# A fused stage whose instruction order comes from a table of places in a turn, one for every occurrence of a step

## The chip, the cores and the metric

The kernel runs on one core of a Trainium2 chip. The metric is device time in microseconds (us) of one execution. Before the change the median of three runs is 1330.56 us (1325.54 to 1330.76).

Five engines take part, each with its own queue of instructions that it works off strictly in the order in which the program lists them: PE (matrix products, with PEld for its weight loads), DVE (vector), ACT (activation), POOL (GpSimd) and SP, which here only issues DMAs. An instruction that waits for another engine holds up all that stands behind it in its own queue. So the order of each queue, which is what this change sets, is part of the program and not of its computation.

## The reference, cut to what matters

The input `x` is 128 sequences of 64 tokens of 256 features. Two layers follow, each with a residual.

```python
h  = scan(gated recurrence over 64 steps of x)              # layer 0, first part
x  = x + ffn_int8(h)                                        # gate, up, silu, int8 fake quant, down
# layer 1, per token row of 256, hyperbolic geometry
xn = layer_norm(logmap0(x)); xm = expmap0(xn * (1 + sc) + sh)
q, k, v = plin(xm, w_q), plin(xm, w_k), plin(xm, w_v)       # 16 heads of 16, 64 x 64 scores
y  = mobius_add(x, expmap0(g * logmap0(attention(q, k, v))))
z  = mobius_add(y, expmap0(g2 * logmap0(plin(plin(modulated layer_norm(y), w_f1), w_f2))))
x  = x + fp6_quant(z) @ fp6_quant(weight).T + bias
```

Norms, `tanh` and `artanh` of a row are one number per row, so a large share of the instructions are chains of tiny ones on tiles of 128 x 8.

## The kernel before, in words

The 8192 tokens are 64 tiles of 128 rows. The program has three stages. The recurrence and the weight preparation come first, then the first part of the int8 feed-forward, which writes its product `h` to DRAM, and then the **fused stage**, the function `fused`, which does all the rest. The change touches the fused stage alone.

There the tiles go in 16 groups of 4 (`GT`, `NGR`). For every group five pieces of work are done: `front` (dequantise `h`, down projection, residual: the steps `load.h`, `front.q8`, `front.cast`, `front.mm`, `front.x1`, `front.add`, `stats1`), `norms` (`ln_coeffs`, `modulate`, the scale `chain.su` and `clip_ball`), `attention` (steps `a.*`), `mlp` (steps `m.*`) and `fp6` (steps `f.*`). `tail` closes the attention of one group and the mlp of another one in one set of tiny instructions (`tail_coeffs`, step `chain.tail`), since both have the same form, and `norms` likewise serves an attention group and an mlp group at once.

The loop at the end of `fused` runs turns k = -5 to 18. In turn k it traces `tail(k)`, `norms(k)`, `fp6(k - 3)`, `mlp(k)`, `attention(k + 5)` and `front(k + 6)`. So the loop is software pipelined: turns -5 to -1 fill the pipe, and turns 11 to 18 empty it. Many of the tiles between the pieces have one or two buffers. In PSUM the banks `dn`, `ao`, `ml` and `fp` are single, and `qk` and `sc` are double.

The order of the queues is not the order of the trace. A list scheduler of the language takes, in a simulated time line, among the instructions whose inputs are ready the one with the lowest priority number. `step(name)` sets this number for what is traced next: `base + (turn + 5) * 1800 + RANK[name]`. `RANK` has one number for each of some 80 step names, so all occurrences of a step in a turn (the eight `a.e`, the four `m.mm`) and all their instructions share one number. The scheduler remains free to deviate from it whenever it believes that an instruction isn't ready, and it does so differently in each turn.

Lines that the prediction speaks of: L774 (`q`, the first instruction of `tail_coeffs`), L651 (a power of -0.5 on POOL, `rsqrt`, used by `chain.tail`, `ln_coeffs`, `chain.su`, `chain.cf` and `chain.full`), L779 to L814 (the rest of `tail_coeffs`), L679 to L710 (`ln_coeffs`), L739 and L740 (`modulate` on DVE), L638 (`clip_ball` on DVE), L756 (the gate product on POOL), L764 (the row products `xdot`), L977 and L982 (`a.qk`, `a.va` on POOL), L940 (`a.lo` on DVE), L1064 (`a.proj`), L1163 (`f.add`).

Of the kernel before, what the change touches and what calls it, by code (L numbers as in the profile page):

```python
# [46 lines left out]
GT = 4  # L47
NGR = NTILE // GT

TURN = 1800  # L50
RANK = {"front.q8": 910, "front.cast": 539, "front.mm": -718, "front.x1": -1305, "front.add": 174, "store.x1": 0, "a.turn": -1220, "a.hi": -1577, "a.lo": 495, "a.qkv": 46, "a.qkvcopy": -917, "a.sq": 2253, "a.nh": -44, "chain.h": -8170, "a.qk": -90, "a.va": -90, "a.turnq": -90, "a.qm": -1178, "a.kt": -1474, "a.sc": -90, "a.e": -877, "a.av": -90, "a.raw": -1338, "a.o": 3284, "a.turno": 1011, "a.ot": -3468, "a.wo": 975, "a.proj": -2819, "m.turn": 987, "m.hi": -123, "m.lo": -2161, "m.mm": 1726, "m.dot": -468, "m.copy": 301, "m.a": -355, "f.max": -10889, "f.q": 4682, "f.rnd": -1889, "f.deq": 4033, "f.turn": 167, "f.yt": 4664, "f.mm": 507, "load.ot": 10015, "f.add": -588, "store.out": -58, "x2n": 2724, "own": 641, "load.xt": -636, "chain.su": 4117, "chain.full": -5861, "chain.cf": -1389, "chain.ln": -2069, "chain.tail": -2513, "stats1": 1067, "stats2": 339, "load.mod0": -1252, "load.mod1": -208, "mod0.0": -3294, "mod0.1": -93, "mod0.2": 398, "mod0.3": -712, "mod1.0": 1137, "mod1.1": 2275, "mod1.2": -5509, "mod1.3": 1054, "sqm0": 2326, "sqm1": -1277, "clip0": -1974, "clip1": -1974, "sqt0": 462, "sqt1": -162, "gate0": -1900, "gate1": 755, "sqg0": -808, "sqg1": 4262, "xdot.a": -1630, "xdot.m": 1293, "load.h": -5461, "load.x": 0, "a.sqo": 76, "load.gate0": 3865, "load.gate1": 3539, "comb.a": 708, "comb.m": -2849}

LA, LM = CFG["LA"], CFG["LM"]

# [510 lines left out]
def fused(ctx, tc, a, out_tok, x_tok, L):  # L565
    nc = tc.nc
    V, S, G_, PE = nc.vector, nc.scalar, nc.gpsimd, nc.tensor
# [21 lines left out]
        Q[CFG["q_" + key]].dma_start(out=out, in_=in_)  # L589

    at = [0]
    turn_ = [-LA]
    base = tc.cur_priority + 4000

    def step(name):

        tc.cur_priority = base + (turn_[0] + LA) * TURN + RANK[name]

    def mk(name, n=2 * GT, bufs=CFG["mk"]):

# [11 lines left out]
    def pick(key, g):  # L612

        es = CFG[key]
        if at[0] < CFG["ef"]:
            es = CFG["fill"].get(key, es)
        return es[g % len(es)]
# [51 lines left out]
    def ln_coeffs(mv, xs=None):  # L669


        step("chain.ln")
        k = lambda name, bufs=1: mk(f"{name}ln", bufs=bufs)
        m, v = mv[:, :, 0], mv[:, :, 1]
        x2s, aa = k("x2s", CFG["xs"]), k("lna", CFG["la"])
        t, rn, n_, l1, l2, z, p, far, near, l1q = (
            k(i) for i in ("t", "rn", "n", "l1", "l2", "z", "p", "far", "near", "l1q"))
        S.activation(t, m, AF.Square)
        V.tensor_tensor(t, t, v, ALU.add)  # L679
        if xs is not None:  # L680
            xx, vx = k("xx"), k("vx")
            S.activation(xx, xs, AF.Square)
            V.tensor_tensor(vx, v, xx, ALU.mult)
            V.tensor_tensor(t, t, xx, ALU.mult)
            v = vx
        V.tensor_scalar(x2s, t, float(D), EPS2, ALU.mult, ALU.max)


        V.tensor_scalar(z, x2s, 1.0 / 32.0, None, ALU.min)
        V.tensor_scalar(far, x2s, 1.0 / 32.0, 0.5, ALU.is_ge, ALU.mult)  # L690
        series(p, z, ARTANH)
        rsqrt(rn, x2s, "n")
        V.tensor_tensor(n_, x2s, rn, ALU.mult)
        V.tensor_scalar(n_, n_, MAX_T, None, ALU.min)
        S.activation(l1, n_, AF.Ln, bias=one, scale=1.0)
        S.activation(l2, n_, AF.Ln, bias=one, scale=-1.0)

        V.tensor_tensor(rn, rn, far, ALU.mult)
        S.activation(near, far, AF.Copy, scale=-2.0 * ARTANH[0], bias=ARTANH[0])
        V.scalar_tensor_tensor(p, p, 1.0 / ARTANH[0], near, ALU.add, ALU.mult)  # L700
        V.tensor_tensor(l1, l1, l2, ALU.subtract)
        V.tensor_tensor(l1, l1, rn, ALU.mult)
        V.tensor_tensor(l1, l1, p, ALU.add)

        S.activation(l1q, l1, AF.Square)
        V.reciprocal(t, l1q)
        V.scalar_tensor_tensor(t, t, 1e-6, v, ALU.mult, ALU.add)
        rsqrt(aa, t, "v")
        if xs is not None:
            V.tensor_tensor(aa, aa, xs, ALU.mult)  # L710
        return x2s, aa

# [14 lines left out]
    def modulate(src, nm, aa, which, i0, u, un):  # L727

        for g in range(GT):
            step(f"load.mod{which}")  # L730
            ss = load_ada(which, 0, 2, i0 + g)
            step(f"mod{which}.{g}")
            ug = u[g]
            if pick(f"mod{which}", g) == "G":
                G_.tensor_scalar(ug, src[g], nm[:, g : g + 1], aa[:, g : g + 1], ALU.add, ALU.mult)
                G_.tensor_tensor(ug, ug, ss[:, 1, :], ALU.mult)
                G_.tensor_tensor(ug, ug, ss[:, 0, :], ALU.add)
            else:
                V.scalar_tensor_tensor(ug, src[g], nm[:, g : g + 1], ss[:, 1, :], ALU.add, ALU.mult)  # L739
                V.scalar_tensor_tensor(ug, ug, aa[:, g : g + 1], ss[:, 0, :], ALU.mult, ALU.add)  # L740
            step(f"sqm{which}")
            square_sum(pick(f"sqm{which}", g), f"u{which}", ug, un[:, g : g + 1])

    def clip_ball(u, su, which):

        for g in range(GT):
            step(f"clip{which}")
            scale(pick(f"su{which}", g), u[g], u[g], su[:, g : g + 1])
# [18 lines left out]
    def tail_coeffs(ag2, xg, x2s, xs, own, src, cols):  # L767
# [3 lines left out]
        k = lambda name: mk(f"{name}tc")  # L771
# [22 lines left out]
        V.tensor_tensor(yc, e, r2[:, gt:], ALU.mult)  # L794
        S.activation(y2, e, AF.Square)
        if xs is not None:
            V.tensor_tensor(xg, xg, xs, ALU.mult)
        V.scalar_tensor_tensor(t1, xg, 2.0, yc, ALU.mult, ALU.mult)
        V.tensor_tensor(xy, x2s, y2, ALU.mult)
        V.scalar_tensor_tensor(den, t1, 1.0, xy, ALU.add, ALU.add)  # L800
# [3 lines left out]

        S.activation(t1s, t1, AF.Copy, bias=TINY)
        if xs is not None:
            V.tensor_tensor(t1s, t1s, xs, ALU.mult)
        V.tensor_tensor(s_, t1s, den, ALU.mult)
        if own is not None:
            S.copy(own[:, cols], s_[:, src])  # L810
        V.reciprocal(t1, t1s)
        S.activation(r, x2s, AF.Copy, scale=-1.0, bias=1.0)
        V.tensor_tensor(yc, yc, t1, ALU.mult)
# [39 lines left out]
    def get_mv(k):  # L853

        if k not in mvs:
            step("own")
            mvs[k] = mk("mv", 4 * GT, CFG["mv"]).rearrange("p (g k) -> p g k", k=2)
            if k < 0 or k + LA >= NGR:
                G_.memset(mvs[k], 1.0)
        return mvs[k]  # L860

    def get_tail(k):

        if k not in tails:
            step("own")
            t = tails[k] = mk("ag2", 4 * GT, CFG["tl"]), mk("xg", bufs=CFG["tl"]), mk("x2n", bufs=CFG["tl"])
            if not LM <= k < NGR:
                for v in t:
                    G_.memset(v, 1.0)
        return tails[k]  # L870
# [296 lines left out]
    def norms(k, xs):  # L1167

        on_a, on_m = k + LA < NGR, k >= 0
        mv = mvs.pop(k)  # L1170
        step("chain.ln")
        un, nm = mk("un"), mk("nm")
        if not (on_a and on_m):
            G_.memset(un, 1.0)
        x2n, la = ln_coeffs(mv, xs)
        S.activation(nm, mv[:, :, 0], AF.Copy, scale=-1.0)
        todo = []
        if on_m:
            um = ums[k] = Pairs("u2")
            todo.append((1, k, us[k], um, HM))  # L1180
        if on_a:
            ua = uas[k + LA] = Pairs("u1")
            todo.append((0, k + LA, x1s[k + LA], ua, HA))
        for which, i, x, u, h in todo:
            at[0] = i * GT
            modulate(x, nm[:, h], la[:, h], which, i * GT, u, un[:, h])
            if not CFG["jsu"]:
                clip_ball(u, radial(un[:, h], f"su{which}"), which)
        if CFG["jsu"]:
            su = radial(un, "su")  # L1190
            for which, i, x, u, h in todo:
                clip_ball(u, su[:, h], which)
        step("x2n")
        if on_a:
            G_.tensor_copy(get_tail(k + LA)[2][:, HA], x2n[:, HA])
        if on_m:
            G_.tensor_copy(get_tail(k + LM)[2][:, HM], x2n[:, HM])

    def tail(k):

# [29 lines left out]
            return u, s_[:, HM]  # L1230

    xss = {}
    for pr in range(CFG["hl"]):
        load_h(pr)
    for i in range(CFG["fl"]):
        front(i)
    for k in range(-LA, NGR + LM):
# [13 lines left out]
            fp6(k - LM, *done)  # L1251
        if k + LA + CFG["fl"] < NGR:
            front(k + LA + CFG["fl"])


# [46 lines left out]
```

## Time and profile before

| what | us |
| --- | --- |
| median of three runs | 1330.56 |
| the profiled execution's own time | 1332.73 |
| its span, first to last instruction | 1331.0 |
| DVE busy in the span | 1128.2 |
| PE busy | 1075.1 |
| ACT busy | 847.8 |
| POOL busy | 840.2 |

The profile is of one execution. The fused stage's engine work begins at about 302 us, where the first instructions of `front` start (the first loads of `h` are issued earlier). The turns can be told by L774, which occurs once in each of the turns 0 to 18. It starts at 461.9 us in turn 0 and at 1294.2 us in turn 18. The time axis of the views is microseconds from the span's start, and an engine's idle time before an instruction is put down to the instruction that ended its wait.

### The profile page before, as it was taken

Reading aid. Unit: us, or ns where it says so; the run is one execution under the profiler, and the core shown is the slowest. Engines: PE = TensorE matmul, PEld = TensorE weight load, DVE = VectorE, ACT = ScalarE, POOL = GpSimd, SP = SyncE. Lnnn points to the kernel's source line nnn. Section 1 sums busy time; section 2 is a strip of 40 time slices with the busy share of each in tenths; the row PEclk is TensorE's granted clock in tenths of the full one; section 3 lists DMA queues with packets and bytes.
Section 4 is the critical chain, followed back from the end, with each engine's and each line's share of the span. In section 5 each row is a group of like instructions: output and inputs, shape, how many; then the busy total and the mean of one; then the engine's idle time right before and its main releaser. Section 6 shows DMA issues by size and latency. Waiting matters only on the chain. (4 is left out here: it accounts for less than half of the span.)

```text
span 1331.0 us, 23828 instructions
## 1 busy us (share of the span) xinstructions
PE 1075.1 (81%) x7382; PEld 742.9 (56%) x7404; DVE 1128.2 (85%) x3337; ACT 847.8 (64%) x2607; POOL 840.2 (63%) x1024
## 2 busy tenths in 40 slices
PE   6999977984479798988889788897888988874756
PEld 5766642332356565655666566675666756653534
DVE  5766769995787779899999999999989999799674
ACT  2455547981467677678667776776778867764331
POOL 3110118864787858878968778776686776764541
PEclk9999979995699899899899899998999869986765
DMA  7721105678843314334335245323432223323211
GB/s 240 294 70 59 54 1 201 262 276 255 259 130 106 126 33 143 113 103 146 113 124 155 89 127 159 96 69 120 135 105 80 65 72 96 96 84 91 80 43 52
DMA packets 119304, 163.64 MB, mean 123 GB/s; under 512 B 10885, under 2 KB 72074, under 8 KB 119178
## 3 DMA queue, kind: packets, MB, share of 16 engines
q1 hardware_dynamic: 119178, 162.13, 38.5%
q8 instruction: 58, 0.95, 0.3%
q14 instruction: 68, 0.56, 0.1%
HBM read 115.94 MB, written 46.14 MB: 122 GB/s over the span
## 5 line engine op out<-in xcount | busy, mean ns | idle before, releaser
L629 ACT ACTIVATE junk<-u 128x256 bf16<-128x256 f32 x432 | 182.2, 425 | 102.8 <-POOL u L756 31.4
L950 PE MATMUL qk<-wqkv,uT 128*128 128x512 f32 (+1 forms) x768 | 180.2, 374 | 10.7 <-ACT uT L938 10.5
L756 POOL TENSOR_TENSOR u<-u,ada 128x256 f32<-128x256 f32 x128 | 100.0, 785 | 86.4 <-ACT junk L629 76.3
L950 PEld LDWEIGHTS qk<-wqkv,uT 128*128 128x128 f32 x768 | 126.1, 202 | 46.5 <-issue 17.6
L1007 PE MATMUL sc<-qM,kT 64*64 64x256 f32 x1024 | 126.7, 412 | 10.9 <-ACT kT L996 9.4
L1095 PE MATMUL ml<-wm,uT 128*128 128x512 f32 (+1 forms) x384 | 122.5, 458 | 0.0
L1095 PEld LDWEIGHTS ml<-wm,uT 128*128 128x128 f32 x384 | 84.7, 223 | 51.0 <-issue 14.7
L1026 PE MATMUL ao<-va,e 128*64 128x34 f32 x2048 | 89.5, 240 | 22.0 <-DVE u L1064 13.1
L1026 PEld LDWEIGHTS ao<-va,e 128*64 128x64 f32 x2048 | 78.7, 154 | 50.1 <-DVE u L1064 16.0
L636 ACT ACTIVATE qM<-sc,mhead 128x256 f32<-128x256 f32 x256 | 102.3, 494 | 5.4 <-PE sc L95 5.4
L908 PE MATMUL dn<-wdT,hq 128*128 128x256 bf16 (+1 forms) x384 | 65.1, 310 | 38.6 <-DVE x L911 17.0
L982 POOL TENSOR_TENSOR va<-qkv,comb 64x256 f32<-64x256 f32 x128 | 87.8, 703 | 5.2 <-PE ao L1026 2.7
L629 ACT ACTIVATION_READ_ACCUMULATOR junk<-u 128x1 f32 x432 | 86.8, 201 | 0.0
L977 POOL TENSOR_TENSOR qkv<-qkv,comb 128x512 f32<-128x512 f32 x64 | 72.9, 1157 | 21.2 <-DVE comb L968 17.2
L1007 PEld LDWEIGHTS sc<-qM,kT 64*64 64x64 f32 x1024 | 56.7, 139 | 51.1 <-ACT kT L996 13.8
L445 PE MATMUL pg<-hsT,WT 128*128 128x128 f32 x504 | 76.4, 293 | 8.2 <-ACT hsT L457 7.9
L640 POOL TENSOR_SCALAR hb<-hl,cu 128x1280 int8<-128x1280 f32 (+1 forms) x64 | 64.5, 1013 | 29.1 <-DMA hl<-h_d 11.1
L1158 PE MATMUL fp<-wfT,yT 128*128 128x256 f32 x256 | 81.6, 450 | 0.0
L445 PEld LDWEIGHTS pg<-hsT,WT 128*128 128x128 f32 x504 | 66.1, 195 | 26.6 <-ACT hsT L457 23.4
L1016 ACT ACTIVATE e<-sc 128x512 f32<-128x512 f32 x128 | 74.7, 603 | 7.3 <-PE sc L1007 3.9
L527 POOL TENSOR_TENSOR hv<-uv,sil 128x512 f32<-128x512 f32 x44 | 57.9, 1318 | 29.7 <-ACT sil L521 13.0
L457 ACT ACTIVATE hsT<-gate 128x128 f32<-128x128 f32 x128 | 39.6, 309 | 53.8 <-DVE gate L456 53.8
(287 smaller groups left out, 3176.5 us busy)
## 6 DMA issues: line engine op xcount, KB each, us to landing
ada<-ada_d SPq DMA_DIRECT2D x128, 256.0 KB, 3.6
h_d<-hv SPq DMA_DIRECT2D x80, 256.0 KB, 2.2
hl<-h_d SPq DMA_DIRECT2D x32, 640.0 KB, 4.7
ada<-ada_d SPq DMA_DIRECT2D x128, 128.0 KB, 2.5
xt<-in_xT_dram SPq DMA_DIRECT2D x16, 512.0 KB, 3.7
xr<-in_x_dram SPq DMA_DIRECT2D x32, 256.0 KB, 4.1
x_d<-x SPq DMA_DIRECT2D x32, 256.0 KB, 2.9
xt<-x_d SPq DMA_DIRECT2D x32, 256.0 KB, 3.0
```

The lines of the kernel that those rows point to most:

```text
L445: lp = PE.matmul(pg[c][:, st], lhsT=WT[:, k, c * P : (c + 1) * P], rhs=hp[:, k, :], start=False, stop=False, skip_group_check=True)
L629: S.activation(junk, src, AF.Square, accum_out=acc)
L636: S.activation(dst, src, AF.Copy, scale=by)
L756: ENG[pick(f"gate{which}", g)].tensor_tensor(av, av, gb, ALU.mult)
L950: PE.matmul(pm[:, :n_], lhsT=uT[:, z, k, cs], rhs=wqkv[:, w, k, lo:hi], start=False, stop=(k == 1 and q == 2))
L977: ENG[pick("qks", g)].tensor_tensor(qk, qk, bc_in(comb[:, xy * 48 : xy * 48 + 32], HD), ALU.mult)
L982: ENG[pick("va", g)].tensor_tensor(va[r, :, s, 0:HD], qkv[r, xy, 512:768].rearrange("p (h d) -> p h d", d=HD), bc_in(comb[r, xy * 48 + 32 ...
L1007: PE.matmul(sc[rr][s * T : (s + 1) * T, c * 256 : (c + 1) * 256].rearrange("p (v t) -> p v t", v=4), lhsT=kTs[xy][r, c, s * T : (s + 1) * ...
L1016: S.activation(e.rearrange("p c v t -> p (c v t)"), sc[rr], AF.Exp, scale=1.0 / math.sqrt(HD))
L1026: PE.matmul(pv[xy * T : (xy + 1) * T, hh], lhsT=E[2 * xy + hh // 4][:, c, hh % 4, :], rhs=vas[(2 * h2 + xy) % 4][:, c * 8 + hh], start=Tru ...
L1095: PE.matmul(pm[:, cs], lhsT=uT[:, z, k, i * P : (i + 1) * P], rhs=wm[:, w, k, cs], start=False, stop=(k == 1 and q == 2))
L1158: PE.matmul(o, lhsT=yT[:, 2 * i + c, :], rhs=wfT[:, c, :], start=False, stop=(c == 1))
```

## The change

`RANK` and `TURN` go. In their place stands `PLACE`, which has for every occurrence of a step in a turn (`a.e#0` to `a.e#7`) a list of places, one for each of its instructions. A place is in turns: an instruction of turn k with place 2.405 stands at k + 2.405. Some steps of tiny instructions are split (`ln.x`, `ln.1`, `ln.y`, `ln.m`, `tail.x`, `tail.1`, `tail.y`, `tail.2`, `tail.o`, `tail.3`, `un`), so that each part has its own place. After all has been traced, each engine's instructions (DMA issues of SP included, most memsets left out) are sorted by place, and each is tied to the one before it by an order dependency without a semaphore. So the scheduler has no freedom left in the fused stage: on each engine the order in a turn is the same in every turn. The computation, the tiles, their buffers and the engines of the steps stay as they were.

```diff
-TURN = 1800
-RANK = {"front.q8": 910, "front.cast": 539, "front.mm": -718, ...}
+PLACE = {"a.av#0": [3.41423, 3.41453, ...], ..., "a.proj#3": [4.41393], ..., "chain.tail#0": [-0.4606, -0.38235, -0.2353, -0.2353, -0.235, ...], ...}
...
     def step(name):
-        tc.cur_priority = base + (turn_[0] + LA) * TURN + RANK[name]
+        key = (turn_[0], name)
+        n = times[key] = times.get(key, -1) + 1
+        order.append((len(traced), PLACE.get(f"{name}#{n}", order[-1][1] if order else [0.0]), turn_[0], name, n))
+        tc.cur_priority = base + int((order[-1][1][0] + turn_[0] + 2 * LA) * 4000)
...
+    turn_[0] = -LA - 2
     for pr in range(CFG["hl"]):
         load_h(pr)
+    turn_[0] = -LA - 1
     for i in range(CFG["fl"]):
         front(i)
...
+    queues = {}
+    marks = [*order, (len(traced),)]
+    for (lo, place, k, name, _), (hi, *_) in zip(marks, marks[1:]):
+        own = name in ("un", "own")
+        for j, ins in enumerate(traced[lo:hi]):
+            if (own or type(ins).__name__ != "InstMemset") and type(ins).__name__.startswith("Inst"):
+                queues.setdefault(str(ins.engine), []).append((k + place[min(j, len(place) - 1)], len(queues.get(str(ins.engine), ())), ins))
+    for q in queues.values():
+        q.sort(key=lambda e: e[:2])
+        for (_, _, a_), (_, _, b_) in zip(q, q[1:]):
+            tc.add_manual_dep(b_, a_.name, mybir.DependencyInfo(
+                mybir.DependencyClass.NoSync, mybir.DependencyReason.DATA), reason="order of places")
```

Entries of `PLACE` that the prediction uses (the first number of each, unless more are given): `ln.1#0` starts at 0.484, `ln.y` 0.819, `mod1.2V` 1.029, `chain.su` 1.153, `a.lo#0` 1.446, `chain.h#0` 2.201 to 2.403, `xdot.m#3` 2.509, `gate1#3` 2.480, `a.qk#0` and `#1` 2.405 and 2.419, `a.o#0` 3.518, `a.proj#3` 4.414, `sqg0#3` 4.539, `load.gate0#2` 4.439, `front.q8#1` -1.576, and for `chain.tail` -0.461 (L774), -0.382 (L651) and then -0.2353 to -0.2281 for L779 to L795, `tail.1` -0.232 to -0.186.

## The prediction

> **What bounds the kernel now.** First the busy lines of the page, to see which engine can be the bound.
>
> ```profile
> PE 1075.1 (81%) x7382; PEld 742.9 (56%) x7404; DVE 1128.2 (85%) x3337; ACT 847.8 (64%) x2607; POOL 840.2 (63%) x1024
> ...
> DVE  5766769995787779899999999999989999799674
> ```
>
> DVE is the fullest, and it is full from slice 19 to slice 33, in the middle of the fused stage. Then the busy time by stretch. The cuts are the fused stage's start, `L774` of turns 0, 2, 12 and 15 (1204 us), and the end.
>
> ```profile
> 303.00:462.00 159.00, 111.51 (x775) 73.49 (x776) 121.87 (x300) 82.90 (x231) 116.98 (x152) 0.77 0.61 181
> 462.00:542.00 80.00, 71.63 (x579) 50.29 (x581) 67.80 (x221) 59.53 (x190) 55.71 (x65) 0.87 0.28 85
> 542.00:1090.00 548.00, 469.79 (x3838) 346.05 (x3839) 520.05 (x1565) 407.52 (x1325) 426.02 (x521) 0.92 0.37 112
> 1090.00:1204.00 114.00, 87.20 (x708) 66.60 (x706) 102.48 (x370) 77.74 (x273) 74.57 (x94) 0.93 0.27 86
> 1204.00:1331.00 127.00, 76.88 (x248) 54.67 (x248) 84.08 (x320) 41.46 (x142) 53.78 (x57) 0.62 0.21 65
> ```
>
> The columns are PE, PEld, DVE, ACT, POOL. Length less the DVE column is DVE's idle time: 37.1 and 12.2 in the fill, 28.0 in ten full turns (2.8 a turn of 54.8), 11.5, and 42.9 at the end: 131.7 us in 1028. An order can save only idle time, and 28 is all that the ten full turns hold. What that idle time is:
>
> ```profile
> DVE u L739 <- DMA ada<-ada_d: 6.9, 4, 3.0
> DVE tftc L786 <- ACT zztc L785: 4.3, 4, 2.6
> DVE lnaln L710 <- POOL lnaln L651: 3.8, 4, 1.5
> DVE satc L779 <- POOL r L651: 2.3, 4, 0.9
> DVE rden L1033 <- ACT raw L1030: 1.0, 1, 1.0
> ```
>
> (542 to 1090; total, times, longest.) These are round trips of tiny instructions through ACT and POOL, and late loads. At the end it is the last groups' own chain:
>
> ```profile
> DVE ot L1163 <- PE fp L1158: 15.7, 6, 5.9
> DVE junk L1099 <- PE ml L1095: 8.5, 5, 2.9
> DVE satc L779 <- POOL r L651: 3.8, 2, 2.4
> ```
>
> **The change, part by part.** No instruction, tile or DMA is added or taken out, and the ties have no semaphore, so all that changes is who stands behind whom. I sum by DVE's idle time, stretch by stretch.
>
> *Full turns (542 to 1090).* I sorted DVE's and POOL's steps by the fraction of their places, which gives one turn's order, and put the durations of this trace to it. Recorded DVE durations from 542 to 1090 sum to 626.2 us against 520.05 busy, since records of neighbours overlap, so a DVE stretch takes 0.83 of its sum.
>
> The tightest part starts with `chain.h#0`, whose result (place 2.403) releases `a.qk` on POOL. From there to the first use of the `tail` power, `L779`, the table gives DVE 14.3 us of durations, 11.9 us busy. POOL has in that stretch, in this order, two `a.qk` (1175 ns each), four gate products (787), `front.q8#1` (1451 + 610), the `ln` power (1691), one `a.va` (700) and the `tail` power:
>
> ```profile
> L651 POOL TENSOR_TENSOR r<-q,nhalf 128x16 f32<-128x16 f32 x10 | 30.0, 3001 | 4.8 <-DVE q L774 3.3 <-DVE msc L1132 0.8 <-DVE l1ln L701 0.5
> ```
>
> That is 2350 + 3148 + 2061 + 1691 + 700 + 3001 = 12.95 us, so DVE waits about 1.0 us at `L779` in each turn. Then `L779` to `L794` stand next to one another in the table. `L786` needs an ACT square of `L781`'s result and nothing else stands between: about 0.5 (ACT row 0.22 to 0.31, and two hand-overs). `L706` behind ACT's square likewise, with nothing between, 0.4. `L799` behind ACT's `y2` has one instruction between: 0.2. Sum 2.1 us a turn, 21 in ten turns against 28.0: **-7**.
>
> The other joints have room. `a.proj#3` to `a.o#0` is one `ao` bank through PE, ACT, PE, ACT; a block of `a.av` takes 1.1 us of wall time in this trace and `raw` 0.4, so about 4 us with the `a.qkv` products between, against 6 us of DVE work in the table. `mod1.2V` (1.029) needs its load, 3.6 us, issued after `mod1.0V`'s second half (0.844); between lies 9 us of DVE work. All loads stay on SP; `load.gate0#2` (4.439) stands behind a load whose buffer is free since 0.224. So DMA waits I take at 0 of today's 6.9 in the middle; ends 0 and 14 (twice today's).
>
> *1090 to 1204.* The same order still holds there, 2.1 a turn over two to three turns, with less work: 5 against 11.5: **-6**.
>
> *End.* By time 99 us of DVE durations now stand behind turn 15's `L774` (1204 us); by places 91 us do, as the table has part of mlp 13 ahead of it. Over all turns busy is 896.27 of 1049 summed, 0.854, so 7 us less lie behind that point, while the last group's chain is the same: 127 less 7: **-7** (ends 0, if the chain alone decides, and -15).
>
> *Fill.* Here a fixed order can cost. On DVE, `a.lo#0` of a group (1.446) stands ahead of `ln.1#0` of the next group (1.484). So in turns -5 to -1 a norm can't start until the group before has come through modulate, scale, clip, transpose and `a.lo`. Before, the first `L679` is at 320.0 us and the first `L940` at 356.0: 36 us, but with other groups' work let in between, and the next norms started at 334, 357, 379, 414 and 487. The bare path of such a turn, by rows: two powers 3.3, the `ln` instructions 4, modulate 5, squares 0.8, `chain.su` 2.4, clip 1.4, transpose, `a.hi` and `a.lo` 2: 19, with hand-overs 22 us. So a ramp turn takes 22 to 36 us by this path. I take 29 for the first two, and for the next three what PE and ACT need by the summed work (36, 39, 40): the norm of turn 0 at 320 + 174 = 494 against 487, with about the same DVE work behind it (146 against 150 us of durations): **+6** (ends -10 and +25).
>
> Sum: 1331.0 - 7 - 6 - 7 + 6 = 1317 of span. The profiled execution's own time is 1.7 above its span, and the median of the runs 2.2 below that execution: 1332.7 - 14 - 2.2 = 1316.5, so **1316**.
>
> **A rule against it.** DVE's busy time is itself partly waiting:
>
> ```profile
> L638 DVE TENSOR_SCALAR u<-u,sur x96: 300/350/1407, 350.7 to 1256.0; 128x256 f32<-128x256 f32 x96
> L740 DVE SCALAR_TENSOR_TENSOR u<-u,lnaln,ada x86: 389/485/2747, 333.2 to 1248.8; 128x256 f32<-128x256 f32 x86
> L644 DVE SCALAR_TENSOR_TENSOR pptc<-zztc x19: 110/161/604, 473.4 to 1300.2; 128x8 f32<-128x8 f32 x19
> ```
>
> (shortest, median, longest.) From 542 to 1090 `L638` has a mean of 540 and `L740` one of 635, so over their medians 60 x 0.19 + 50 x 0.15 = 19 us, in a kernel where POOL is busy 426 of 548. The Trainium skill, SBUF — State Buffer, section SBUF: two separate sides, says that the two engines share a port pair which one holds for a whole instruction while the other stands still. By that rule the table's packed `tail` block would run against `a.va` and two `a.qk` on POOL that stand right behind the power, and would grow by up to their 3.5 us a turn, so the sum would be 1351. The rows show such growth in this order too, so I leave DVE's busy time as it is and keep the rule's effect for a rival.
>
> **Rivals.**
>
> *Slower by the ramps (1345).* The ramp path costs its 36 us in every one of the five turns, as it did at 320 to 356, and the first turn with `tail` likewise: the norm of turn 0 at about 511, and the end likewise without its 7: 1316 + 17 + 7 + 5. For it: the rule on DVE above. Against: the 36 us had other work in them. It decides once the path is above some 33 us.
>
> *Slower in the full turns (1350).* POOL's 12.95 against DVE's 11.9 grows by 3 us a turn, by collisions or a PE result late at `va`: 1316 + 10 x 3 + 4. For it: POOL's row above; against: POOL has 122 us idle in the 548.
>
> *No change (1330).* The order comes out nearly the one that the scheduler chose. For it: ordered by the time in a turn, most steps of this trace stand as in the table, only attention's end is 0.4 turn earlier now. Idle time then only moves.
>
> *Much faster (1290).* Both the 2.8 us a turn and a tenth of the 19 us and their like (all DVE instructions of two inputs) fall, and the fill too: 1316 - 26.
>
> **How the numbers follow.** Chances: forecast 0.38, much faster 0.13, no change 0.16, ramps 0.19, full turns 0.14. About 0.5% is what a measurement of this kernel can tell from no change, 1324 to 1337. So faster 0.51, same 0.16, slower 0.33. The forecast's own range is 1302 to 1324. Both signs hold much, so the range goes from 1284 to 1352.
>
> **What would show it.** Right: `L774` of turns 2 to 12 evenly spaced at 53 to 54 us, DVE idle under 25 us there, its longest wait `L779` behind POOL's power; `L679` of turn 0 between 485 and 500; fewer than 125 us from turn 15's `L774` to the end. Wrong: unevenly spaced turns, over 40 us idle in the ten turns, `L679` of turn 0 past 505, or a DVE busy time that differs by over 15 us from 896, which would mean that collisions with POOL and not waits decide.

## The result and the profile after

The changed kernel takes 1364.67 us (median of 4 runs, 1363.19 to 1367.99) against 1330.12 us (4 runs, 1325.54 to 1330.76) beside it: a ratio of 1.0271, 95% interval 1.024 to 1.0302. It is slower, by 35 us, where 1316 was forecast, with a range from 1284 to 1352. The profiled execution took 1367.99 us, with a span of 1365.9.

The busy lines of the page, PE to POOL, and DVE's row of the 40 slices:

```profile
PE 1093.9 (80%) x7370; PEld 735.9 (54%) x7404; DVE 1129.2 (83%) x3337; ACT 857.0 (63%) x2607; POOL 837.5 (61%) x1024
...
DVE  5766679995765889989999999999999998888763
```

DVE has the same work as before (1129.2 against 1128.2 us busy), so nearly the whole 35 us is time in which DVE stands idle. Where, by the same five stretches (cut at `tail`'s first instruction, now `L780`, of turns 0, 2, 12 and 15; columns PE, PEld, DVE, ACT, POOL; idle is the length less the DVE column):

```profile
303.00:464.00 161.00, 106.66 (x717) 68.61 (x721) 105.07 (x269) 78.20 (x215) 100.89 (x136) 0.76 0.44 136
464.00:556.00 92.00, 75.56 (x656) 53.02 (x656) 78.93 (x241) 66.13 (x206) 71.07 (x87) 0.89 0.41 121
556.00:1113.00 557.00, 486.33 (x3741) 341.62 (x3750) 527.17 (x1586) 408.91 (x1312) 426.10 (x518) 0.90 0.37 115
1113.00:1247.00 134.00, 107.58 (x807) 78.14 (x802) 110.71 (x384) 87.59 (x300) 80.96 (x106) 0.83 0.26 81
1247.00:1366.00 119.00, 57.65 (x218) 41.73 (x216) 75.13 (x292) 38.37 (x132) 47.61 (x48) 0.73 0.20 62
```

| stretch | idle before | idle after | difference | forecast |
| --- | --- | --- | --- | --- |
| fill, to turn 2's `tail` | 37.1 + 12.2 | 55.9 + 13.1 | +19.7 | +6 |
| ten full turns | 28.0 | 29.8 | +1.8 | -7 |
| turns 12 to 15 | 11.5 | 23.3 | +11.8 | -6 |
| after turn 15's `tail` | 42.9 | 43.9 | +1.0 | -7 (in length) |

The last stretch is 8 us shorter, as forecast and for the reason forecast: 9.0 us of DVE work were done ahead of it (75.13 us busy against 84.08). But this work takes its time in the stretch before, where DVE is busy for 8.2 us more (110.71 against 102.48). So nearly all of the loss is at the two ends of the pipeline, and the full turns, which the forecast gave a gain, gained nothing. Their +1.8 is no loss that can be told: twelve kernels of this document have the changed order in these turns (all but `e4`, `e8` and `e11`), and their ten turns hold from 25.0 to 32.7 us of idle time, one profile each.

PE's granted clock is not the reason: at 0.871 to 0.875 the four executions of the changed kernel took 1363.19 to 1367.99 us, and five executions of the kernel before at 0.872 to 0.875, timed beside the experiments, 1332.32 to 1336.27.

The waits of DVE in the fill (303 to 556 us; total, times, longest):

```profile
DVE x L923 <- DMA xr<-in_x_dram: 9.6, 2, 7.1
DVE u L745 <- DMA ada<-ada_d: 9.4, 4, 3.7
DVE x L921 <- POOL u L741: 9.2, 2, 4.6
DVE nh L968 <- ACT sq L966: 8.5, 7, 2.3
```

No single wait carries the stretch: two loads, a buffer that POOL gives back late, and a square of ACT have nearly the same share. After turn 12 (1113 to 1366 us) it is the same picture:

```profile
DVE ot L1173 <- PE fp L1168: 12.1, 5, 4.4
DVE junk L1109 <- PE ml L1105: 9.8, 8, 2.1
DVE u L1120 <- POOL cfr L669: 8.1, 6, 1.9
DVE junk L770 <- POOL u L762: 6.2, 7, 1.5
DVE u L1152 <- ACT y L1148: 5.4, 4, 2.5
```

The lower three are readers that wait for a chain through POOL or ACT, at the same place of the order in each turn. They sum to 19.7 us. In the kernel before (1090 to 1331 us) the same three sum to 4.0:

```profile
DVE junk L764 <- POOL u L756: 1.8, 2, 1.2
DVE u L1110 <- POOL cfr L666: 1.3, 4, 0.6
DVE u L1142 <- ACT y L1138: 0.9, 1, 0.9
```

What stands between a producer and its reader can be counted. For `L1120` it is the DVE instructions between the last `m.dot` (`L1109`) and the first `m.a` (`L1120`), where POOL's `cfr` has to be made:

| turn (by time) of the changed kernel | 2 to 8 | 9 to 11 | 12 | 13, 14 | 15, 16 | 17 |
| --- | --- | --- | --- | --- | --- | --- |
| DVE instructions between | 10 | 8, 7, 7 | 4 | 3, 3 | 1, 1 | 0 |
| idle before `L1120`, us | 0 to 0.13 | 0.13 | 0.91 | 0.91, 1.05 | 1.71, 1.66 | 1.90 |

Those that go missing belong to `front`, to attention and to `clip_ball`, as there are no more groups for them. In the kernel before, the scheduler still put 6 to 18 instructions there in turns 12 to 17, and the idle time was at most 0.59 us.

### The profile page after: what moved, and what is told of

It is laid out like the page before. It is cut to its first block, busy times and chain, and to the rows that moved or that the text cites. A ratio compares the mean times of both kernels' runs of the same rounds, so it can differ in the third digit from the quotient of the medians.

```text
span 1365.9 us, 23764 instructions
## 1 busy us (share of the span) xinstructions
PE 1093.9 (80%) x7370; PEld 735.9 (54%) x7404; DVE 1129.2 (83%) x3337; ACT 857.0 (63%) x2607; POOL 837.5 (61%) x1024
## 3 DMA queue, kind: packets, MB, share of 16 engines
q1 hardware_dynamic: 119178, 162.13, 37.1%
## 4 chain that ended last, share of the span: by engine, by line
DVE 46%; PE 29%; POOL 10%; issue 6%; ACT 5%; DMA 3%; SPq 0%; POOLq 0%; DVEq 0%; ACTq 0%
PE pg L444 5%; PE qk L960 4%; PE sc L1017 3%; DVE u L830 3%; PE pg L425 3%; DVE junk L770 2%; DVE am L529 2%; PE dn L918 2%; DVE u L1120 2%; DVE u L745 2%; DVE hv L528 2%; DVE nh L968 2%; PE ao L1069 2%; PE ml L1105 2%; PE ao L1036 1%
## 5 line engine op out<-in xcount | busy, mean ns | idle before, releaser
L960 PE MATMUL qk<-wqkv,uT 128*128 128x256 f32 (+1 forms) x768 | 201.2, 383 | 3.6 <-ACT uT L948 3.6
L1017 PE MATMUL sc<-qM,kT 64*64 64x256 f32 x1024 | 133.0, 453 | 15.7 <-ACT kT L1006 12.6
L918 PE MATMUL dn<-wdT,hq 128*128 128x256 bf16 (+1 forms) x384 | 90.3, 322 | 36.4 <-DVE x L921 13.9
L639 ACT ACTIVATE qM<-sc,mhead 128x256 f32<-128x256 f32 x256 | 106.1, 491 | 13.8 <-PE sc L94 13.7
L1036 PEld LDWEIGHTS ao<-va,e 128*64 128x64 f32 x2048 | 81.9, 158 | 47.7 <-ACT raw L1040 13.0
L1036 PE MATMUL ao<-va,e 128*64 128x34 f32 x2048 | 93.2, 244 | 15.5 <-ACT raw L1040 12.3
L1105 PEld LDWEIGHTS ml<-wm,uT 128*128 128x128 f32 x384 | 84.1, 228 | 30.6 <-issue 11.9
L1144 POOL TENSOR_TENSOR u<-u,mrc 128x512 f32<-128x512 f32 x32 | 36.7, 1165 | 98.4 <-DVE mrc L1141 98.4
L992 POOL TENSOR_TENSOR va<-qkv,comb 64x256 f32<-64x256 f32 x128 | 83.4, 661 | 15.3 <-PE ao L1036 11.8
L987 POOL TENSOR_TENSOR qkv<-qkv,comb 128x512 f32<-128x512 f32 x64 | 68.0, 1083 | 30.2 <-DVE comb L978 23.1
L963 ACT COPY qkv<-qk 128x512 f32<-128x512 f32 (+1 forms) x128 | 63.1, 508 | 34.6 <-PE qk L960 34.3
L94 PE MATMUL fp<-ident,u 128*128 128x128 f32 x128 | 30.7, 357 | 61.1 <-DVE ot L1173 57.4
L526 POOL TENSOR_TENSOR hv<-uv,sil 128x512 f32<-128x512 f32 x44 | 57.7, 1314 | 31.4 <-DVE am L529 14.5
```

The source lines that it names most:

```text
L639: S.activation(dst, src, AF.Copy, scale=by)
L918: PE.matmul(py[:, i * D : (i + 1) * D], lhsT=hq[r, j, i * P : (i + 1) * P], rhs=wdT[r, j, :], start=(i == 0 and j == 0), stop=(j == 5), sk ...
L960: PE.matmul(pm[:, :n_], lhsT=uT[:, z, k, cs], rhs=wqkv[:, w, k, lo:hi], start=False, stop=(k == 1 and q == 2))
L987: ENG[pick("qks", g)].tensor_tensor(qk, qk, bc_in(comb[:, xy * 48 : xy * 48 + 32], HD), ALU.mult)
L992: ENG[pick("va", g)].tensor_tensor(va[r, :, s, 0:HD], qkv[r, xy, 512:768].rearrange("p (h d) -> p h d", d=HD), bc_in(comb[r, xy * 48 + 32 ...
L1017: PE.matmul(sc[rr][s * T : (s + 1) * T, c * 256 : (c + 1) * 256].rearrange("p (v t) -> p v t", v=4), lhsT=kTs[xy][r, c, s * T : (s + 1) * ...
```

## The experiments

Each kernel was timed beside the kernel before; ratios are to that, and idle times are by the same stretches. The expectations call the engines VectorE (DVE), ScalarE (ACT), GpSimd (POOL), TensorE (PE) and SyncE (SP).

**SyncE alone (`e1`).** The loads come late in the fill (`xr` above), and all DMAs are in SyncE's order.

```diff
-    for q in queues.values():
+    for eng, q in queues.items():
+        if eng.endswith("SP"):
+            continue
```

> The changed kernel with the ties left out on SP alone (DMA issues), so that the scheduler orders the loads and stores by priority. Theory Q (the fill loses its 19 us because the loads of x, h and the modulation rows stand in a fixed file on SP, the first load of x 10 us later than before): about 1350, with the first L923 add no longer waiting 7 us for xr and L682 of turn 0 near 488. Theory C (the fill loses because the compute engines go by the steady order, above all a.lo of a group ahead of the next group's ln.1): no gain in the fill, 1360 to 1368. Neither expects anything in the full turns; the drain's 13 us more of DVE idle time stay in both.

1369.74 us, ratio 1.0293 (1.0243 to 1.0342). The first `xr` load is issued at 301 us instead of 312 and DVE no longer waits for it (it waits 4.9 us for a later one), but the idle time to turn 0 is 63.0 us instead of 55.9: other waits took its place. The order of the DMAs alone isn't the cause.

**The fill without ties (`e2`), and the end without ties (`e3`).** Places remain as priorities there.

```diff
+        q = [e for e in q if e[0] >= 1.5]      # e2: fill free
+        q = [e for e in q if e[0] < 11.5]      # e3: end free
```

> The ties hold only among instructions with a place of 1.5 or more, so the fill (turns -7 to 1) is ordered by the scheduler on all engines, SP too, with priorities from the places. Theories Q and C both expect the fill's loss to go: DVE idle before turn 2's tail back from 69 to about 50 us, so about 1346. If it stays above 1360, the fill's loss is not in the ties but in the places used as priorities, or is given back later.

> The ties hold only among instructions with a place under 11.5, so the drain is ordered by the scheduler with priorities from the places. Theory D (the drain loses 13 us because one turn's order, made for 55 us of DVE work a turn, leaves DVE waiting for POOL's scale, gate and power when a turn has less): about 1352, with the DVE waits on L669, L762 and L654 after 1110 us mostly gone. Rival (the drain's loss is the later start of its last groups, which the fill passes on): 1362 to 1367.

1352.37 us, ratio 1.0164 (1.0116 to 1.0212), and 1352.37 us, 1.0149 (1.0093 to 1.0206). Each brings back 12 us, each in its own stretch. In `e2` the idle time to turn 0 is 40.0 us instead of 55.9, but 6.0 of these 15.9 us are lost again up to turn 2, so that 59.1 us stand there where some 50 were expected. In `e3` the idle time from turn 12 on is 15.6 + 37.7 us instead of 23.3 + 43.9, in a profiled execution of 1343.70 us, 8.7 below the median. The three readers above wait 4.7 us there (`L1120` 1.0, `L770` 2.4, `L1152` 1.3) instead of 19.7, while the wait for POOL's power (`L785`), which had been expected to go too, is 6.4 us against 5.3. The ties cost time at both ends.

**No ties at all (`e4`).**

```diff
-        for (_, _, a_), (_, _, b_) in zip(q, q[1:]):
+        for (_, _, a_), (_, _, b_) in ():
```

> No ties at all: the places serve only as priorities for the scheduler. If the ties are what costs in the ramps, this has both gains: 1330 to 1340, near the kernel before. If the table's order itself is worse than the old ranks even as a priority, it stays over 1355. If the ties are worth something in the full turns, the ten full turns' DVE idle time rises from 30 us by what they were worth.

1348.91 us, ratio 1.015 (1.0088 to 1.0211), between the two times expected. The stretches of the profile, from turn 0's `tail` on:

```profile
463.00:539.00 76.00, 70.22 (x582) 49.34 (x584) 66.22 (x199) 58.20 (x181) 50.95 (x60) 0.92 0.29 89
539.00:1107.00 568.00, 488.48 (x3729) 357.43 (x3736) 522.85 (x1612) 405.50 (x1320) 428.99 (x520) 0.89 0.36 110
1107.00:1237.00 130.00, 108.36 (x852) 78.78 (x852) 110.51 (x388) 89.28 (x305) 83.80 (x107) 0.89 0.27 81
```

The full turns now hold 45.1 us of idle time, against 29.8 with ties and 28.0 with the old ranks. So the ties do save 15 us in the full turns, but only of what the places cost when they serve as priorities alone.

**Both ends free (`e5`)**, and then one engine's share of it (`e6`, `e7`).

```diff
+        q = [e for e in q if 1.5 <= e[0] < 11.5]                 # e5: every engine; e6: if DVE; e7: if not DVE
```

> Ties only among places from 1.5 to 11.5, on every engine; before and after that, places are priorities. Freeing the fill alone gave 1352.4 us, freeing the end alone 1352.4, the change as it is 1364.7. Theory 1, two separate losses at the two ends: both come back, 1352.4 + 1352.4 - 1364.7 = 1340 us (1336 to 1344), with some 40 us of VectorE idle time from 303 us to turn 0's tail and some 15 after turn 12. Theory 2, what one end gives the other takes (a start that is earlier only meets a later wait): no better than either alone, 1350 to 1354. On either, the ten full turns keep some 26 to 30 us of idle time, so that the sum stays over the kernel before by what is left in them and at the two ends.

> Only VectorE is freed in the two ramps (its ties kept among places from 1.5 to 11.5); ScalarE, GpSimd, TensorE and SyncE keep all of theirs. Theory V, VectorE's own fixed order costs the ramps (work that is ready stands behind an instruction that waits): VectorE alone brings back most of the 24 us, so 1340 to 1346 us. Theory O, VectorE gets its work late because the other engines' orders send it late: under a third comes back, 1357 to 1365 us.

> The other way about: in the two ramps VectorE keeps its ties, and ScalarE, GpSimd, TensorE and SyncE are freed. Theory V (VectorE's own order costs): under a third of 24 us comes back, 1357 to 1365 us. Theory O (the others' orders cost): most of it, 1340 to 1346 us. If both this and the kernel with VectorE freed come near 1352, the loss is shared: a fixed order on either side is enough to keep half of it.

Both ends free give 1339.86 us, ratio 1.0119 (1.0056 to 1.0183): the two losses add, as theory 1 had it, and the end's idle time (15.8 + 37.2 us) and that of its three readers (4.7) are those of `e3`. With only VectorE free it is 1377.09 us (1.0406, 1.0342 to 1.0471), with all but VectorE free 1391.71 us (1.0514, 1.0427 to 1.0602). Both theories on one engine fall: each half is slower than the whole change. The fill of the kernel with only VectorE tied:

```profile
303.00:472.00 169.00, 113.89 (x749) 76.34 (x750) 101.01 (x276) 82.00 (x221) 101.35 (x142) 0.73 0.47 145
472.00:574.00 102.00, 81.29 (x620) 56.89 (x619) 70.61 (x235) 64.55 (x201) 68.03 (x81) 0.83 0.29 88
```

68.0 and 31.4 us of idle time. In these two kernels the orders of the engines belong together: the scheduler's order on some engines with the table's on the others costs more than either.

**The packed small instructions (`e8`).** After the change the small gaps of DVE in the ten full turns are larger (those up to 0.3 us sum to 16.8 us, before to 6.0) and the large ones smaller (13.0 against 22.0). Four places are moved to put independent work between dependent instructions.

```diff
-"mod1.1V#0": [0.72771, ..], "xdot.a#3": [-0.43108], "xdot.m#3": [2.5087], "tail.x#0": [-0.43078]
+"mod1.1V#0": [0.7374, ..], "xdot.a#3": [-0.2347], "xdot.m#3": [2.7663], "tail.x#0": [-0.23245]
```

> All ties kept; four places of VectorE's table are moved so that independent work stands inside the chain of small instructions: one modulation (mod1.1V) into the ScalarE round trip of 0.27 us ahead of L711, one sum of products (xdot.a#3) into the one of 0.27 us ahead of L792, a second (xdot.m#3) between two dependent small ones, and tail.x next to its reader. Theory G, the gaps that the packed order leaves between dependent small instructions are lost time in every full turn: 0.27 + 0.27 and some 0.1 of ends that don't overlap come off each turn, so ten full turns lose 5 to 7 us of idle time, and with the turns at the ends the kernel comes to 1356 to 1360 us. Theory S, the gaps are slack and something else sets the turn (another engine, a transfer): the idle time moves to other waits, 1363 to 1367 us.

1366.49 us, ratio 1.0324 (1.0263 to 1.0386). The small gaps fall from 16.8 to 10.8 us (16.5 to 17.6 in the twelve kernels with the changed order in these turns). The ten turns' idle time is 26.3 instead of 29.8 us, which lies within the 25.0 to 32.7 of those twelve: `L785` now waits for POOL's power (3.6 us in 6 of the turns, none before), and the whole kernel gains nothing that shows. Theory S is nearer: what sets the turn is not these gaps.

**The step that the prediction named (`e9`, `e12`, `e13`).** In turns below 0 the front and the norm of the next group are put ahead of this group's attention.

```diff
+        if turn_[0] < 0 and name.startswith(NORM):     # front, load.h, load.x, stats1, store.x1, chain.ln, ln., un, load.mod0, mod0, sqm0
+            place = [p - EARLIER for p in place]       # e9: 0.3; e12: 0.1; e13: 0.3, sqm0 left out
```

> All ties kept. In the turns below 0 the steps of the front and of the norm (front, load.h, load.x, stats1, store.x1, chain.ln, ln, un, load.mod0, mod0, sqm0) get places 0.3 of a turn earlier, so that in the fill the next group's norm stands ahead of this group's attention in every engine's order instead of behind it. Theory N, the step that the prediction named (the next group's norm behind this group's attention) is what costs the fill: of the 15 us that came back there when the fill was untied, at least 8 come back here, 1350 to 1357 us. Theory B, the fill's waits are for things that the norm's own steps free (x and ada buffers, the xr load behind them on SyncE), which a common shift leaves as they are: 3 us at most, 1361 to 1368 us.

> The same move as e9 (front and norm ahead of attention in turns below 0, all ties kept), by 0.1 of a turn instead of 0.3, which took 1391.5 us. Theory K, the named cause is right in direction and 0.3 went too far: 1355 to 1361 us, under the change's 1364.7. Theory L, any common move of these steps ahead of attention costs, so the next group's norm standing behind attention is not what the fill loses by: 1366 to 1378 us, between 0 and 0.3 of a turn.

> As e9 (0.3 of a turn, 1391.5 us), but ScalarE's squares of the modulated rows (sqm0) stay at their own places; in e9 ScalarE waited 29 us in the fill for the rows that they read (junk behind u of GpSimd and VectorE), with the attention's squares behind them on its queue, for which VectorE's nh then waited 26.0 us. Theory H, one instruction placed ahead of its operand holds an engine's whole queue, and that was e9's loss: the two waits go, 1364 us or less, and 1350 to 1357 us if the norm's place was also the fill's loss. Theory L, the loss of e9 is in another step: 1380 us or more.

1391.5 us (ratio 1.0476, 1.044 to 1.0511), 1382.83 us (1.0389, 1.0341 to 1.0437) and 1394.22 us (1.048, 1.044 to 1.0519): all slower than the change, all in the fill (idle time to turn 0's `tail`: 79.6, 73.7 and 81.9 us against 55.9). So nothing is gained by putting the norm ahead of attention in this way. It isn't the exact reverse of the step that was named, as all steps of front and norm in the turns below 0 move together and turn 0's norm does not: in `e9` the norms of turns -4 to -1 do come earlier (459.0 us against 459.5 for the last, up to 8 us for the others), and turn 0's comes at 528.6 instead of 505.4. ACT's waits up to turn 0's `tail` are, in `e9`:

```profile
ACT junk L637 <- POOL u L748: 16.8, 4, 5.3
ACT junk L637 <- DVE u L751: 12.6, 6, 3.4
```

and in `e13`, where the squares of the modulated rows (`sqm0`, the `junk` above) were left in their place:

```profile
ACT nm L1193 <- DVE mv L728: 31.9, 4, 11.0
```

Once the squares don't hold ACT's queue, another instruction of the norm does (9.1 of its 31.9 us are in `e9` and in the change too), and attention's squares stand behind that one. A wait taken from one head of a queue came back at another.

**A pair apart at the end (`e10`).** From turn 10 on, seven steps of the second half of an MLP go 0.09 of a turn earlier.

```diff
+        if turn_[0] >= 10 and f"{name}#{n}" in SECOND:   # m.mm, m.dot, m.copy of rows 2 and 3, chain.cf
+            place = [p - 0.09 for p in place]
```

> All ties kept. From turn 10 on, seven steps of the second MLP matmul half (m.mm, m.dot and m.copy of rows 2 and 3, chain.cf) get places 0.09 of a turn earlier, so that f.add#1, f.deq and their like stand between the producer m.dot#3 and its reader m.a#0 in VectorE's order. Theory A, the end loses time because in turns without attention a producer and its reader stand next to each other in the order: the six waits of m.a#0 behind GpSimd's cfr (8.1 us after 1113 us) go, and with them 4 to 8 us, 1357 to 1361 us. Theory C, the waits are a chain's own latency and come back at the next place (m.dot#2 behind TensorE, f.deq behind ScalarE): 1363 to 1367 us.

1374.65 us, ratio 1.0355 (1.0316 to 1.0394). The waits of DVE from turn 12 on:

```profile
DVE junk L1113 <- PE ml L1109: 18.7, 10, 6.8
DVE ot L1177 <- PE fp L1172: 11.6, 6, 4.6
DVE junk L774 <- POOL u L766: 9.1, 10, 1.4
```

The 8.1 us behind POOL's `cfr` are gone, and 8.9 us more stand one step earlier, behind PE's `ml`, whose reader was moved earlier as well. So this pair, put apart by a shift of its producer, gained nothing. Theory C holds as to the waits; its number was too low, since the stretch from turn 12 to 15 grew by 11 us.

**The memsets (`e14`)**, tied by the change as well.

```diff
-        own = name in ("un", "own")
+        own = False
```

> All ties kept but those of GpSimd's own and un memsets, which read nothing and which the scheduler puts early when it may (own comes 64 us of GpSimd work earlier in the kernel whose fill is free). Theory U, these tied memsets hold GpSimd's queue in the fill: the first turns come 3 us or more earlier, 1355 to 1361 us. Theory Z, they cost nothing: 1362 to 1367 us.

1364.92 us, ratio 1.0262 (1.0226 to 1.0297): no part in it.

**The old ranks as priorities, ties in the middle (`e11`)**, with the four moved places of `e8`.

```diff
-        tc.cur_priority = base + int((order[-1][1][0] + turn_[0] + 2 * LA) * 4000)
+        tc.cur_priority = base + (max(turn_[0], -LA) + LA) * TURN + RANK[old]
...
+        q = [e for e in q if 1.5 <= e[0] < 11.5]
```

> The kernel before's table of ranks gives the priorities again, and ties by place hold only among places from 1.5 to 11.5, with the four moved places that open VectorE's packed chain. Theory 1, the loss of what was left after untying the ramps (some 9 to 16 us) lies in the places as priorities there, and the ties are worth a little in the full turns: the ramps come to the lengths of before (159, 80 and some 241 us after turn 12), and ten full turns to 23 to 26 us of idle time against 27.9 before, so 1325 to 1331 us, no measurable difference from the kernel before. Theory 2, the seams between the free and the tied part cost by themselves: 1335 us or more.

1331.14 us (12 runs), ratio 1.0023 (1.0 to 1.0045), no difference that can be told. The first three stretches of its profile:

```profile
303.00:458.00 155.00, 108.58 (x754) 71.65 (x754) 116.59 (x294) 82.05 (x228) 113.58 (x145) 0.75 0.59 176
458.00:541.00 83.00, 72.03 (x638) 51.57 (x634) 67.00 (x219) 61.90 (x194) 57.80 (x69) 0.92 0.24 76
541.00:1100.00 559.00, 488.89 (x3760) 343.06 (x3757) 530.50 (x1594) 405.79 (x1312) 432.25 (x521) 0.89 0.37 115
```

With the scheduler and its old ranks at the ends all of the 35 us are back, but for what can't be told. From turn 12 on the three readers wait 1.1 us. The tied middle has 28.5 us of idle time, as much as the kernel before has without ties (28.0), so theory 1 missed there: the table isn't better in the full turns. None of these kernels beats the kernel before.

## Why the prediction was wrong

- **The step that failed most is the end: the full turn's idle time was taken over for turns that are not full.** "The same order still holds there, 5 against 11.5: -6" for turns 12 to 15 measured +11.8, an error of 18 us. The order does hold there, but three readers whose round trips are covered in a full turn lie bare (19.7 us against 4.0 after turn 12's `tail`), as fewer instructions of other groups stand ahead of them (counted for one of the three, from 10 down to none). Freeing the order at the end takes their waits to 4.7 us, the old ranks there to 1.1.
- **A term was counted as saved that only moves.** "7 us less lie behind that point: -7" is right as to the last stretch. But DVE's work stays the same, so these 7 us have to be done ahead of that point, and the sum has no term for them; in idle time the last stretch measured +1.0. The other three terms alone give 1324 us of span.
- **Fill: "+6" measured +19.7, with the path right and its start wrong.** The order that was named is seen: each of the five norms starts as `a.lo#0` (`L950`) of the group before ends, as here, and from the first norm to turn 0's it took 175.3 us where the sum has 174 (166.9 before).

```profile
380.76 0.68 DVE L950 TENSOR_TENSOR uT<-qk,uT 128x512 fp32r<-128x512 f32 x1
381.36 0.73 DVE L682 TENSOR_TENSOR tln<-tln,mv 128x8 f32<-128x8 f32 x1
```

  But the sum left the first norm at its old 320.0 us, and it starts at 330.1, so that turn 0's norm comes at 505.4, against 494 forecast and 486.9 before. Of these 10.1 us 2.3 were there before the fused stage began; 7.8 are lost in `front`, which the table orders too. The first lines are of the changed kernel, the last is of the one before:

```profile
308.55 0.69 DVE L921 TENSOR_TENSOR x<-dn,sdh 128x512 f32<-128x512 f32 x1 [0.84 <-PE dn L918]
316.37 0.69 DVE L923 TENSOR_TENSOR x<-x,xr 128x512 f32<-128x512 f32 x1 [7.13 <-DMA xr<-in_x_dram]
330.09 0.35 DVE L682 TENSOR_TENSOR tln<-tln,mv 128x8 f32<-128x8 f32 x1
```

```profile
320.00 0.17 DVE L679 TENSOR_TENSOR tln<-tln,mv 128x8 f32<-128x8 f32 x1 [0.28 <-ACT tln L678]
```

  From the last DVE instruction ahead of the stage to the first norm it takes 20.0 us before and 27.8 in the change; 18.1 to 18.8 with all engines free in the fill (`e2`, `e4`, `e5`), 20.9 with DVE free (`e6`), 25.3 with all but DVE free (`e7`) and 27.8 with SP free (`e1`). So DVE's own order has the larger part of this loss, though freeing DVE alone costs more later. That the ramp turns could be made shorter by another order of the norm and attention is not shown: the one move that was tried cost time in three kernels. No single pair was found that carries the fill's loss.
- **Full turns: -7 measured +1.8.** The 21 us of idle time forecast lie under the 25.0 to 32.7 of all twelve kernels with this order. By the waits of the changed kernel (556 to 1113 us):

```profile
DVE tln L711 <- ACT l1qln L710: 3.7, 10, 1.2
DVE u L1152 <- ACT y L1148: 3.4, 6, 0.7
DVE tftc L792 <- ACT zztc L791: 2.8, 10, 0.3
DVE junk L1109 <- PE ml L1105: 1.9, 1, 1.9
```

  Of the four named waits `L706` (now `L711`) came as forecast (0.37 a turn against 0.4), `L786` (now `L792`) at 0.28 against 0.5, and the other two not at all: POOL's power (2.91 us) ends 0.1 us ahead of DVE's reader in nine of the ten turns, after a DVE stretch of 13.0 to 15.8 us where 11.9 was worked out. The error was to take the four waits for all the idle time of a turn, and every other gap at nothing. Gaps of up to 0.1 us alone, some 35 ns between one small instruction and a dependent next one, sum to 8.8 us (before 4.4), and waits in other parts of the turn, as the second and fourth line, make up the rest.
- **Right:** the turns are evenly spaced (`L780` of turns 2 to 10 is 55 to 59 us apart, before 35 to 77), but at 56 us and not at 53 to 54; DMA waits in the full turns are gone (6.9 us before); the end after turn 15's `tail` is 119 us, under the 125 named, which tells nothing of the whole, as the work was only moved; and DVE's busy time in the fused stage, 897 against 896, says that collisions didn't decide. Of the signs of being wrong, `L679` of turn 0 past 505 came (505.4). An even turn isn't a shorter one: the ten turns took 557 us, before 548, with 7 us more DVE work in them.
- **The rivals.** The ramps' rival (1345) had the right place and too small a price: it gave the fill 17 us more and the rest 12, and had no term for turns 12 to 15. Its reason, a path of 36 us in each ramp turn, is not what made turn 0's norm late: the turns took what the forecast gave them, and the late start came instead. The full turns' rival (1350) fell: POOL's 12.95 us were not late.

## What to carry to other kernels

An order made from the steady turn of a software pipeline should be held only in that turn: here it gained nothing there and cost some 32 of 1330 us of idle time at the fill and the end, where the neighbours that cover its round trips go missing. That reason is shown for the end; in the fill it is the late start and the path of the ramp turns that the runs show. Judge such a table by the idle time of the bounding engine per stretch, ends apart from the middle, and don't count work that only moves as saved. Change all engines' orders together: half a table was slower than the whole (1377 and 1392 against 1365). A wait at the head of an in-order queue that was moved away by a shift of one block came back at another place in `e1`, `e10` and `e13`, so a shift is worth a try only where something else is ready to stand there.

## What the runs showed of the hardware

Four small DVE instructions of `tail` end just after the POOL instruction that runs beside them, and last up to six times as long as at their shortest. DVE's and then POOL's time line in turn 7 of the changed kernel (start, length, engine, line):

```profile
845.27 0.60 DVE L785 TENSOR_SCALAR satc<-r 128x8 f32<-128x8 f32 x1
845.79 0.15 DVE L786 TENSOR_TENSOR nntc<-q,r 128x8 f32<-128x8 f32 x1
845.98 1.03 DVE L787 TENSOR_TENSOR nntc<-nntc,satc 128x8 f32<-128x8 f32 x1
847.28 0.75 DVE L792 TENSOR_SCALAR tftc<-zztc 128x8 f32<-128x8 f32 x1 [0.27 <-ACT zztc L791]
848.06 0.54 DVE L793 TENSOR_SCALAR zztc<-zztc 128x8 f32<-128x8 f32 x1
```

```profile
845.22 0.62 POOL L992 TENSOR_TENSOR va<-qkv,comb 64x256 f32<-64x256 f32 x1
845.92 2.08 POOL L987 TENSOR_TENSOR qkv<-qkv,comb 128x512 f32<-128x512 f32 x2
847.96 0.61 POOL L992 TENSOR_TENSOR va<-qkv,comb 64x256 f32<-64x256 f32 x1
```

`L785` ends at 845.87, POOL's `va` at 845.84. `L787` ends at 847.00, the first of the two `qkv` products (1.06 us each) at 846.98; `L792` at 848.03, the second at 848.00; `L793` at 848.60, `va` at 848.57. In 39 of the 40 cases of the ten full turns these four end 0.02 to 0.03 us after a POOL product. At their shortest in the same kernel they take 0.157 (`L785`), 0.166 (`L787`) and 0.171 us (`L792`, `L793`). This agrees with the Trainium skill, SBUF — State Buffer, section SBUF: two separate sides, which the prediction weighed: the pair of ports that the two share is held by one engine for a whole instruction. The page says so of DVE instructions with two SBUF inputs, as `L787`, or in a two-port mode; whether the three `TENSOR_SCALAR` run in such a mode no run here shows. But it had been so before, spread over other instructions of `tail` (the ten turns' `tail` instructions have 72.6 us of durations before and 69.6 after), so it is no part of the difference. In a packed chain a duration of 0.6 us can thus hold a wait that no view of idle time shows.
